# A flamingo layer stack on one core: the block-scale products of two roundings on GpSimd instead of VectorE

## The chip, the core and the metric

The kernel runs on one core of one Trainium2 chip. The metric is the device time of one execution in microseconds. The engines are named as the profile names them: PE is TensorE's matmul (PEld its weight load), DVE is VectorE, ACT is ScalarE, POOL is GpSimd, SP is SyncE, which here only issues DMAs.

## What is computed

Four layers in a row on 2048 tokens (4 x 512) of width 512, each with a residual and a tanh gain:

```python
x = x + tanh(g_xattn[0]) * L0_xattn(layernorm(x), token ids, ctx, ctx, ctx)   # 4 experts by token id
x = x + tanh(g_ffn[0])   * L0_ffn(layernorm(x), w_gate, w_up, w_down)          # block-float FFN
x = x + tanh(g_xattn[1]) * L1_xattn(layernorm(x), ctx, ctx, gamma)             # 8 heads of attention
x = x + tanh(g_ffn[1])   * L1_ffn(layernorm(x), ...)                           # 64-expert top-6 MoE
```

The change lies in the second layer. Its weights and its activations are rounded in blocks of 32 along the last axis:

```python
amax  = max(abs(block))                     # of 32 elements
scale = exp2(floor(log2(amax)) - 2)
q     = clip(round_to_tiny_float(block / scale), -max_norm, max_norm) * scale
...
gate, up = q_act(x) @ q_w(w_gate).T, q_act(x) @ q_w(w_up).T
out      = q_act(silu(gate) * up) @ q_w(w_down).T
```

The last step of either rounding, "times scale", is what is moved.

## The kernel before

The program has four stages that follow one another in time. In each of the first three, tiles are of 128 tokens and the order of the instructions on PE, ACT and DVE is the order in which the code emits them (a schedule written by hand); in the first two stages this holds for POOL's queue too[...].

**First layer and the rounding of weights (about 0 to 250 us).** Tokens are sorted by expert into 19 tiles. A loop over i (lines 531 to 558) transposes, multiplies with the context (`times_context`, L473), gates on DVE (`gated`, L485: one operand in SBUF, one in PSUM), scales on ACT (L489) and scatters the rows by an indirect DMA that POOL issues (`add_rows`, L490). For the first eight i, POOL also issues a gather (`take`, L441). Beside this, the generator `quantize` (from L240) rounds 24 blocks of weights of 128 x 1024, and each block is ten DVE instructions and a cast on ACT: a reduce to the block maxima (L247), two small integer operations on 128 x 32 (L249, L251), the division by the scale (L255), two operations for the exponent (L258, L260), two for rounding (L262, L265), the clamp (L268), and the product with `wide`, the scale spread over the block in bf16 by ACT at L253 (L270). The generator yields an assumed cost after every step, and `some_weights(us)` takes steps until that budget is used up: twice 3.6 us in each pass of the loop, some more ahead of it, and what is left after it. A block that is done goes into `rounded`, from which PE transposes it (L206 or L221) in a later `turn_weights`. So the yields decide where on DVE's queue a block's steps lie between the loop's L485.

**FFN in block float (about 250 to 515 us).** 16 tiles. For tile j, DVE does `times_up` (L655) for four quarters, and `block_scales` and `block_round` for three pieces: the two halves of the hidden row (128 x 1024, called a0 and a1 here) and the next tile's normalized row h (128 x 512). `block_scales` is a reduce (L586) and two small operations (L587, L589), with a cast on ACT (L591); `block_round` is a product with the inverse scale into fp8 (L602), the clamp (L608) and the product with the scale (L609). PE transposes each piece (`turned`, L621), ACT copies it out of PSUM (L622), and then PE multiplies: `gate_up` (L641), `down` (L661). After a1 of three of the tiles, DVE also does `factors_from` (L158 and a chain of small operations). POOL issues one DMA per tile (L667).

The order on DVE in a tile is: L655 x2, scales and rounding of a0, scales and rounding of the next h, L655 x2, scales and rounding of a1.

**Attention and routing (about 515 to 850 us), MoE (about 850 us to the end).** The change touches no instruction of these. The attention stage starts when the FFN's buffers are free, and the first loads of expert weights (L756 to L759) are issued inside it. In the attention stage POOL has some small arithmetic of its own: L905 to L908 on 128 x 1, L1028 and L1034 on 128 x 64.

Of the kernel before, what the change touches and what calls it, by code (L numbers as in the profile page):

```python
# [14 lines left out]
ALU = mybir.AluOpType  # L15
# [31 lines left out]
def flamingo_kernel(  # L47
# [21 lines left out]
    nc = tc.nc  # L69
# [115 lines left out]
    with (  # L185
# [43 lines left out]
        sources, rounded = deque(), deque()  # L229

        def fetch_weights(n):
            for _ in range(n):
                if left:
                    f, args = left.popleft()
                    sources.append(f(*args))

        def quantize():


            n = 2 * D  # L240
            nb = n // BLK
            magic = 1.5 * 2.0 ** (23 - 1)
            while sources:
                src, turn = sources.popleft()
                s3 = src.rearrange("p (k b) -> p k b", b=BLK)
                top = qp.tile([P, nb], F32, name="mx_top")
                nc.vector.tensor_reduce(top, s3, AX.X, ALU.max, apply_absolute_value=True)  # L247
                yield 1.21
                nc.vector.tensor_scalar(top.bitcast(I32), top.bitcast(I32), EXP_MASK, None, ALU.bitwise_and)  # L249
                inv = qp.tile([P, nb], F32, name="mx_inv")  # L250
                nc.vector.tensor_scalar(inv.bitcast(I32), top.bitcast(I32), -1.0, float(254 << 23), ALU.mult, ALU.add)  # L251
                wide = qp.tile([P, n], BF16, name="mx_wide")
                nc.scalar.copy(wide.rearrange("p (k b) -> p k b", b=BLK), top.unsqueeze(2).to_broadcast([P, nb, BLK]))  # L253
                yield 0.36
                nc.vector.tensor_tensor(s3, s3, inv.unsqueeze(2).to_broadcast([P, nb, BLK]), ALU.mult)  # L255
                yield 1.22
                e = qp.tile([P, n], F32, name="mx_e", bufs=1)
                nc.vector.tensor_scalar(e.bitcast(I32), src.bitcast(I32), EXP_MASK, None, ALU.bitwise_and)  # L258
                yield 0.69
                nc.vector.tensor_scalar(e, e, 0.25, None, ALU.max)  # L260
                yield 0.69
                nc.vector.scalar_tensor_tensor(src, e, magic, src, ALU.mult, ALU.add)  # L262
                yield 1.22
                q = qp.tile([P, n], BF16, name="w_q", bufs=3)
                nc.vector.scalar_tensor_tensor(q, e, -magic, src, ALU.mult, ALU.add)  # L265
                fetch_weights(1)
                yield 1.22
                nc.vector.tensor_scalar(q, q, 1.5, -1.5, ALU.min, ALU.max)  # L268
                yield 0.5
                nc.vector.tensor_mul(q, q, wide)  # L270
                rounded.append((turn, q))
                yield 0.69

        left = deque(blocks)
        weights = quantize()
# [24 lines left out]
        with tc.tile_pool(name="route0", bufs=1) as rp:  # L300
# [88 lines left out]
            wide = [P, NT, NS]  # L389
# [6 lines left out]
            for j in range(0, NT, 4):  # L396
                wide = [P, 4, P]
# [56 lines left out]
        def turned(i, what, name):  # L454
            a = stages[i].pop(what)
            ps = ps_t.tile([P, KC, P], F32, name="l0_ps", tag="t")
            for k in range(KC):
                nc.tensor.transpose(ps[:, k, :], a[:, bass.ts(k, P)], ident)
            aT = wp.tile([P, KC, P], F32, name=name)
            nc.scalar.copy(aT, ps)  # L460
            stages[i][name] = aT
# [102 lines left out]
    with (  # L564
# [10 lines left out]
        def load(j):  # L575
            xt = fp.tile([P, D], F32, name="xt", bufs=9)
            nc.sync.dma_start(xt, x_rows[bass.ts(j, P), :])
            stages[j]["x"] = xt

        def block_scales(j, what, n):  # L580

            nb = n // BLK
            src = stages[j][what]
            s3 = src.rearrange("p (k b) -> p k b", b=BLK)
            top = fp.tile([P, nb], F32, name="mx_top", tag=f"mx_top{nb}")
            nc.vector.tensor_reduce(top, s3, AX.X, ALU.max, apply_absolute_value=True)  # L586
            nc.vector.tensor_scalar(top.bitcast(I32), top.bitcast(I32), EXP_MASK, None, ALU.bitwise_and)  # L587
            inv = fp.tile([P, nb], F32, name="mx_inv", tag=f"mx_inv{nb}")
            nc.vector.tensor_scalar(inv.bitcast(I32), top.bitcast(I32), -1.0, float(250 << 23), ALU.mult, ALU.add)  # L589
            wide = fp.tile([P, n], BF16, name="mx_wide", tag=f"mx_wide{n}")  # L590
            nc.scalar.copy(wide.rearrange("p (k b) -> p k b", b=BLK), top.unsqueeze(2).to_broadcast([P, nb, BLK]))  # L591
            stages[j]["mx", what] = inv, wide

        def block_round(j, what, n):

            nb = n // BLK
            src = stages[j].pop(what)
            inv, wide = stages[j].pop(("mx", what))  # L600
            q = fp.tile([P, n], F8, name="mx_q", tag=f"mx_q{n}", bufs=1)
            nc.vector.tensor_tensor(  # L602
                q.rearrange("p (k b) -> p k b", b=BLK), src.rearrange("p (k b) -> p k b", b=BLK),
                inv.unsqueeze(2).to_broadcast([P, nb, BLK]), ALU.mult, saturate=False,
            )
            most = 7.5 / 64.0
            c = fp.tile([P, n], BF16, name="mx_c", tag=f"mx_c{n}")
            nc.vector.tensor_scalar(c, q, most, -most, ALU.min, ALU.max)  # L608
            nc.vector.tensor_tensor(c, c, wide, ALU.mult)  # L609
            stages[j]["q", what] = c  # L610

        def normal(j):
# [16 lines left out]
        def turned_hidden(j, half):  # L629
            if half == 0:  # L630
                stages[j]["iT"] = fp.tile([P, FI // P, P], BF16, name="iT")
            n = FI // 2
            turned(j, ("a", half), n, ps_a, stages[j]["iT"], half * (n // P))

        def gate_up(j, c):
            hT = stages[j]["hT"]
            got = []
            for wT in (wgT, wuT):
                ps = ps_g.tile([P, 512], F32, name="gu", tag="g")
                for k in range(KC):  # L640
                    nc.tensor.matmul(ps, hT[:, k, :], wT[:, k, bass.ts(c, 512)], start=k == 0, stop=k == KC - 1)  # L641
                got.append(ps)
            stages[j]["gu", c] = got

        def silu(j, c):

            half = c // 2
            if c % 2 == 0:
                stages[j]["a", half] = fp.tile([P, FI // 2], F32, name="inter")
            part = stages[j]["a", half][:, bass.ts(c % 2, 512)]  # L650
            nc.scalar.activation(part, stages[j]["gu", c][0], AF.Silu, scale=16.0)

        def times_up(j, c):
            part = stages[j]["a", c // 2][:, bass.ts(c % 2, 512)]
            nc.vector.tensor_mul(part, part, stages[j].pop(("gu", c))[1])  # L655

        def down(j):
            iT = stages[j].pop("iT")
            y = ps_y.tile([P, D], F32, name="y")
            for c in range(FI // P):  # L660
                nc.tensor.matmul(y, iT[:, c, :], wdT[:, c, :], start=c == 0, stop=c == FI // P - 1)  # L661
            stages[j]["y"] = y
# [42 lines left out]
        for j in range(NT):  # L705
            more = j + 1 < NT

            if j:
                turned_hidden(j - 1, 1)
            times_up(j, 0)  # L710
            times_up(j, 1)
            gate_up(j, 2)
            silu(j, 2)
            block_scales(j, ("a", 0), half_n)
            block_round(j, ("a", 0), half_n)
            gate_up(j, 3)
            silu(j, 3)
            if j:
                down(j - 1)
            if j + 8 < NT:  # L720
                load(j + 8)
            sums_of(j + 6)
            if j + 2 < NT:
                normal(j + 2)
            if more:
                block_scales(j + 1, "h", D)
                block_round(j + 1, "h", D)
            if j:
                add_rows(j - 1)
            if more:  # L730
                turned_rows(j + 1)
            turned_hidden(j, 0)
            if more:
                gate_up(j + 1, 0)
                silu(j + 1, 0)
            times_up(j, 2)
            times_up(j, 3)
            block_scales(j, ("a", 1), half_n)
            if more:
                gate_up(j + 1, 1)  # L740
                silu(j + 1, 1)
            block_round(j, ("a", 1), half_n)
            factors_from(j + 3)
# [28 lines left out]
    with (  # L772
# [304 lines left out]
        for n in range((NT + 5) * KC):  # L1077
            j, i = divmod(n, KC)
            turn = ((n - 1) // KC, (n - 1) % KC)
# [185 lines left out]
```

## Time and profile before

| | us |
|---|---|
| median of 3 runs | 1281.77 (1279.57 to 1284.02) |
| the profiled execution: its own time | 1287.6 |
| the profiled execution: span from first to last instruction | 1285.6 |
| busy in the span: PE / DVE / ACT / POOL | 1021.9 / 784.5 / 575.1 / 404.4 |
| mean granted TensorE clock | 0.922 |

Single instructions of the profile that the text refers to, in us: the product of a 128 x 1024 block on DVE 0.69 (L270 and L609), of a 128 x 512 row 0.42 (L609); a reduce of 128 x 1024 1.22; an indirect scatter's issue on POOL 2.1 in the mean (L490), a gather's 1.06 (L441).

How to read it: busy time is the time in which an engine had an instruction running. An average over the whole span says little here, since each stage has another limit; the tables by stage, the timeline of one tile and the waits say which engine is the last to be ready in a stage.

### The profile page before, as it was taken

What the parts mean: (1) busy time and instruction counts of PE and PEld (TensorE: products, weight loads), DVE (VectorE), ACT (ScalarE), POOL (GpSimd) and SP (SyncE); (2) the same over time, 40 slices, a digit from 0 to 9 for tenths busy, and PEclk for the clock granted to TensorE, in tenths of its full rate; (3) what the DMA queues carried; (4) which work ended last, traced back from release to release, by engine and by line L of the source; (5) the groups of instructions that cost most, each with busy time, mean ns of one, the idle gap of its engine ahead of it and who ended that gap; (6) DMA issues with size and microseconds to landing.
All of it is one profiled execution on the core that took longest, in us unless ns stands there. A gap on an engine that the chain in (4) does not pass through costs nothing. (4 is left out here: it accounts for less than half of the span.)

```text
span 1285.6 us, 14848 instructions
## 1 busy us (share of the span) xinstructions
PE 1021.9 (79%) x4603; PEld 524.6 (41%) x4603; DVE 784.5 (61%) x1965; ACT 575.1 (45%) x1144; POOL 404.4 (31%) x554
## 2 busy tenths in 40 slices
PE   4498889358878888588999999994499999999930
PEld 3244444123433333244455555452255555554410
DVE  7799999769999997547677776664122222222200
ACT  3766665366767564456565656551011111111100
POOL 3033312100000000013454535357244544444324
PEclk9799999769999998689999999997699999999975
DMA  9844444311111111972222222129699999999978
GB/s 329 296 102 112 93 96 82 85 31 33 33 17 18 19 23 17 267 209 59 64 64 68 52 60 43 44 38 243 165 286 276 278 276 270 272 265 274 275 199 137
DMA packets 78109, 178.94 MB, mean 139 GB/s; under 512 B 13280, under 2 KB 14320, under 8 KB 77968
## 3 DMA queue, kind: packets, MB, share of 16 engines
q1 hardware_dynamic: 51696, 128.04, 32.8%
q0 software_dynamic: 25504, 49.35, 21.3%
q8 instruction: 37, 0.61, 0.2%
q10 hardware_dynamic: 832, 0.62, 0.2%
q14 instruction: 40, 0.33, 0.1%
HBM read 133.76 MB, written 48.40 MB: 142 GB/s over the span
## 5 line engine op out<-in xcount | busy, mean ns | idle before, releaser
L1174 PE MATMUL gu_ps<-e_gu,gT 128*96 128x384 f32 x512 | 178.5, 492 | 3.5 <-DMA e_gu<-in_L_ffn_w_up_dram 2.2
L836 DVE TENSOR_REDUCE low<-at_s 128x2 f32<-128x1024 f32 x64 | 78.1, 1222 | 87.8 <-PE at_s L831 85.5
L845 ACT ACTIVATE p<-at_s,low 128x512 f32<-128x512 f32 x128 | 86.8, 684 | 87.6 <-DVE low L836 72.4
L1178 DVE SCALAR_TENSOR_TENSOR a<-s,xg,gu_ps 96x192 f32<-96x192 f32 x64 | 35.1, 548 | 147.0 <-ACT s L1176 144.7
L1197 PE MATMUL e_y<-e_dn,eaT 96*96 96x512 f32 x256 | 120.5, 592 | 0.5 <-ACT e_o L1199 0.5
L125 POOL DMA_INDIRECT taken<-token_no,to_i x96 | 97.2, 1013 | 46.8 <-issue 24.7
L1174 PEld LDWEIGHTS gu_ps<-e_gu,gT 128*96 128x96 f32 x512 | 79.2, 165 | 66.6 <-issue 63.7
L1176 ACT ACTIVATE s<-gu_ps 96x192 f32<-96x192 f32 x64 | 20.9, 326 | 178.0 <-PE gu_ps L1174 175.3
L1166 DVE COPY gT<-g_ps 128x384 f32<-128x384 f32 x64 | 35.6, 558 | 104.1 <-PE g_ps L1164 66.8
L667 POOL DMA_DIRECT2D x_rows<-y_sb x16 | 13.9, 868 | 260.6 <-ACT y_sb L666 260.6
L1151 POOL DMA_INDIRECT xg<-h_rows,idx x64 | 59.6, 931 | 93.9 <-DVE a L1178 62.0
L490 POOL DMA_INDIRECT x_rows<-y_sb,to_row x19 | 40.5, 2132 | 147.7 <-ACT y_sb L489 147.7
L831 PE MATMUL at_s<-c_tile,q 64*128 64x512 f32 x256 | 75.6, 670 | 13.7 <-DMA c_tile<-in_ctx_dram 13.7
L856 ACT COPY pT<-p_ps 128x512 f32<-128x512 f32 x128 | 70.1, 591 | 34.5 <-PE p_ps L855 34.2
L855 PE MATMUL p_ps<-ident,p 128*128 128x128 f32 x512 | 72.9, 281 | 14.1 <-ACT pT L856 12.1
L855 PEld LDWEIGHTS p_ps<-ident,p 128*128 128x128 f32 x512 | 57.7, 142 | 61.1 <-issue 26.4
L641 PEld LDWEIGHTS <-hT 128*128 128x128 bf16 x512 | 49.7, 101 | 69.6 <-issue 11.9
L1199 ACT COPY e_o<-e_y 96x512 f32<-96x512 f32 x64 | 37.2, 581 | 89.8 <-PE e_y L1197 84.2
L641 PE MATMUL gu<-wgT,hT 128*128 128x512 bf16 x256 | 70.1, 399 | 6.4 <-ACT hT L622 6.4
L473 PE MATMUL l_mm<-cT,hT 128*128 x152 | 70.9, 610 | 1.7 <-ACT hT L460 1.7
L473 PE MATMUL l_mm<-cT,sT 128*128 x152 | 72.1, 618 | 0.0
L641 PE MATMUL gu<-wuT,hT 128*128 128x512 bf16 x256 | 68.2, 390 | 1.9 <-DVE inter L655 1.9
(227 smaller groups left out, 2026.4 us busy)
## 6 DMA issues: line engine op xcount, KB each, us to landing
e_gu<-in_L_ffn_w_gate_dram SPq DMA_DIRECT2D x64, 384.0 KB
e_gu<-in_L_ffn_w_up_dram SPq DMA_DIRECT2D x64, 384.0 KB
e_dn<-in_L_ffn_w_down_dram SPq DMA_DIRECT2D x64, 384.0 KB
w_src<-in_L_ffn_w_gate_dram SPq DMA_DIRECT2D x8, 512.0 KB
c_sb<-in_ctx_dram SPq DMA_DIRECT2D x4, 1024.0 KB
w_src<-in_L_ffn_w_up_dram SPq DMA_DIRECT2D x8, 512.0 KB
more_rows<-zeros SPq DMA_DIRECT2D x16, 256.0 KB
w_src<-in_L_ffn_w_down_dram SPq DMA_DIRECT2D x8, 512.0 KB
```

What stands on the lines that cost most here:

```text
L125: ins = nc.gpsimd.indirect_dma_start(out=table[:, :], out_offset=bass.IndirectOffsetOnAxis(ap=to, axis=0), in_=what, in_offset=None)
L473: nc.tensor.matmul(ps.unsqueeze(1), aT[:, k, :], cT[:, bass.ds(at + k, 1), :], start=k == 0, stop=k == KC - 1)
L490: nc.gpsimd.indirect_dma_start(out=x_rows[:, :], out_offset=bass.IndirectOffsetOnAxis(ap=to_row[:, i : i + 1], axis=0), in_=y_sb[:, :], in ...
L641: nc.tensor.matmul(ps, hT[:, k, :], wT[:, k, bass.ts(c, 512)], start=k == 0, stop=k == KC - 1)
L831: nc.tensor.matmul(s[:, h, :], t["q"][rows, bass.ts(i, P)], t["c"][rows, :], start=True, stop=True)
L836: nc.vector.tensor_reduce(low, tiles[j]["s", i], AX.X, ALU.max, negate=True)
L845: nc.scalar.activation(p[:, h, :], s[:, h, :], AF.Exp, bias=low[:, h : h + 1], accum_out=t["sums"][:, i, h : h + 1])
L855: nc.tensor.transpose(ps[:, k, :], p[:, h, bass.ts(k, P)], ident)
L856: nc.scalar.copy(tiles[j]["pT"][h][:, :, bass.ts(i, P)], ps)
L1151: nc.gpsimd.indirect_dma_start(out=g[:, :], out_offset=None, in_=h_rows[:, :], in_offset=bass.IndirectOffsetOnAxis(ap=idx[:, e : e + 1], a ...
L1174: nc.tensor.matmul(ps, gT[:, k, :], gu[:, :, k, :], start=k == 0, stop=k == KC - 1)
L1197: nc.tensor.matmul(y, aT[:, c, :], dn[:, c, :], start=c == 0, stop=c == 1)
```

## The change

Both products with the block scale are issued by GpSimd (`nc.gpsimd`) instead of VectorE. In the weights' generator the product no longer has a yield of its own (the 0.69 goes), so a block counts 7.11 where it counted 7.80, and it is emitted together with the clamp. In the FFN loop the transposes of the second half of the tile before, `turned_hidden(j - 1, 1)`, are emitted on PE after `gate_up(j, 2)` instead of at the head of the tile.

```diff
                 nc.vector.tensor_scalar(q, q, 1.5, -1.5, ALU.min, ALU.max)
+
+                nc.gpsimd.tensor_mul(q, q, wide)
+                rounded.append((turn, q))
                 yield 0.5
-                nc.vector.tensor_mul(q, q, wide)
-                rounded.append((turn, q))
-                yield 0.69
...
             nc.vector.tensor_scalar(c, q, most, -most, ALU.min, ALU.max)
-            nc.vector.tensor_tensor(c, c, wide, ALU.mult)
+
+            nc.gpsimd.tensor_tensor(c, c, wide, ALU.mult)
             stages[j]["q", what] = c
...
-            if j:
-                turned_hidden(j - 1, 1)
             times_up(j, 0)
             times_up(j, 1)
             gate_up(j, 2)
             silu(j, 2)
+            if j:
+                turned_hidden(j - 1, 1)
             block_scales(j, ("a", 0), half_n)
             block_round(j, ("a", 0), half_n)
```

In the built program the order on the engines moves with it. POOL's queue in the first stage holds five products ahead of the first scatter, and then mostly one product per pass, between the scatters and gathers. On DVE the blocks of weights lie earlier against the loop: the last L485 comes after the last clamp L268, where before the change 2 blocks and more of rounding followed the last L485.

## What was predicted

> **What bounds the kernel now.** I read the table of busy times by stage first, then the groups of the first stage, then DVE's timeline in one FFN tile, then GpSimd's own arithmetic. The columns of the first table are stretch and length in us, then busy us of PE, PEld, DVE, ACT and POOL (each with a count), granted clock, DMA share, GB/s.
>
> ```profile
> 72.00:250.00 178.00, 150.16 (x574) 76.07 (x572) 167.90 (x267) 106.16 (x192) 49.46 (x27) 0.97 0.39 88
> 250.00:515.00 265.00, 202.55 (x1088) 94.72 (x1088) 226.18 (x438) 163.71 (x256) 13.63 (x16) 0.92 0.17 31
> 515.00:850.00 335.00, 292.17 (x1510) 158.20 (x1511) 222.70 (x782) 196.96 (x470) 126.59 (x279) 0.96 0.35 91
> 850.00:1285.60 435.60, 342.86 (x1274) 172.71 (x1272) 113.18 (x329) 70.63 (x157) 200.38 (x201) 0.90 0.94 239
> ```
>
> In the first stage DVE is busy 167.9 of 178 us (94%), PE 150; in the FFN, 226 of 265 with start and end included, and over 37 of every 40 us in the middle. The other two stages have other limits and follow the FFN's end, so what the first two lose or gain passes to the end one for one.
>
> ```profile
> L247 DVE TENSOR_REDUCE mx_top<-w_src 128x32 f32<-128x1024 f32 x19 | 23.0, 1213 | 0.0
> L255 DVE TENSOR_TENSOR w_src<-w_src,mx_inv 128x1024 f32<-128x1024 f32 x19 | 23.3, 1225 | 0.7
> L260 DVE TENSOR_SCALAR mx_e<-mx_e 128x1024 f32<-128x1024 f32 x20 | 13.9, 694 | 0.7
> L270 DVE TENSOR_TENSOR w_q<-w_q,mx_wide 128x1024 bf16<-128x1024 bf16 x20 | 13.9, 693 | 2.1
> ```
>
> The reader is to see 693 ns, what a block's product costs DVE, and that L260 takes about half of L255's time for as many f32 elements.
>
> ```profile
> 352.15 0.69 DVE L608 TENSOR_SCALAR mx_c<-mx_q 128x1024 bf16<-128x1024 fp8e4 x1
> 352.95 0.69 DVE L609 TENSOR_TENSOR mx_c<-mx_c,mx_wide 128x1024 bf16<-128x1024 bf16 x1
> 353.56 0.68 DVE L586 TENSOR_REDUCE mx_top<-h 128x16 f32<-128x512 f32 x1
> 354.27 0.17 DVE L587 TENSOR_SCALAR mx_top<-mx_top 128x16 int32<-128x16 int32 x1
> ...
> 355.42 0.43 DVE L608 TENSOR_SCALAR mx_c<-mx_q 128x512 bf16<-128x512 fp8e4 x1
> 355.95 0.42 DVE L609 TENSOR_TENSOR mx_c<-mx_c,mx_wide 128x512 bf16<-128x512 bf16 x1
> 356.29 1.28 DVE L655 TENSOR_TENSOR inter<-inter,gu 128x512 f32<-128x512 f32 x2
> ```
>
> DVE runs back to back: a tile takes 14.07 us (from L586 at 343.54 to L586 at 357.61), and 3.3 us more where the statistics chain L158 to L165 follows. With the gap ahead of it, a 1024-wide product occupies 0.80 of the tile, the 512-wide one 0.5.
>
> **What GpSimd takes, and what the two engines do to each other.**
>
> ```profile
> L905 POOL TENSOR_TENSOR r_t<-r_y x48: 192/193/194, 555.7 to 869.9; 128x1 f32<-128x1 f32 x48
> L1034 POOL TENSOR_TENSOR count<-count,chosen x14: 313/315/784, 611.4 to 879.9; 128x64 f32<-128x64 f32 x14
> ```
>
> ```profile
> 865.31 0.74 DVE L894 TENSOR_TENSOR x_tile<-x_tile,r 128x512 f32<-128x512 f32 x1
> 865.44 0.78 POOL L1034 TENSOR_TENSOR count<-count,chosen 128x64 f32<-128x64 f32 x1
> ```
>
> From 1 to 64 elements GpSimd's two-input operation grows by 122 ns, 1.94 ns an element, so 1024 elements are worked out at 193 + 1023 x 1.94 = 2.2 us and 512 at 1.2 us. The Trainium skill (GPSIMD Engine Reference, 3.1 Elementwise) states 4497 ns for 2048 f32, half of which is 2.25 us; the two agree. No bf16 product on POOL is in this trace. The last fence is the one meeting in it of a DVE operation with both inputs in SBUF and a GpSimd product: the latter, usually 0.31 us, took 0.78 and ended 0.17 after DVE's. The skill (SBUF — State Buffer, Who interferes with whom) says why: GpSimd's only port pair is DVE's second one, taken for a whole instruction, and whoever comes second waits, if DVE's is a two-port mode or has two SBUF inputs and GpSimd reads SBUF. A reduce and an operation with a PSUM input stay free. The reverse direction, DVE held by GpSimd, this trace doesn't show at any length. Which operations are in a two-port mode: VectorE: DVE Perf Modes, Mode 2×_2P, gives it to single-source SBUF operations; L260's 694 against L255's 1225 ns agrees. So of a weight block's remaining nine instructions only L247 is free of GpSimd, in the FFN only L586 and L655, and L485 in the first stage.
>
> **The change, part by part.**
>
> *First stage.* Removed from DVE: 24 x 0.73 us (0.693 and a gap) = 17.5. Added: 24 products on POOL, each from 0.15 (the handover of L1007 to L1034) to 2.35 us after the clamp's end. Behind the clamp DVE's queue has, by the built order: in 16 blocks L247 (1.25 us) and then a two-port operation, so DVE stands 1.1 us in each, 17.6; in 6 blocks also L485, cover 1.9, 0.45 each, 2.7; in one L158 at once, 2.3; in the last one nothing. Together 22.6. POOL's queue: where the clamp follows L485 closely, the product lies behind the scatter L490 (2.2 us, its row is ready with L485) and for early i the gather L441 (1.0), starts up to 2 us late and meets L249 to L258 rather than L247; I put some 4 us on this (0 to 10). Stalls 26.6. Cheaper yields also put the last L485 behind the last clamp; before, 20 us of rounding followed it and hid its path. Now that path is bare: L485's transposes 0.7, copy 0.6, weights' transposes 0.6, product with the context 2.6 to 3.5, L489 0.7, L490 2.2, handovers, landing (2, an estimate from the gap of 2.7 us between the loads' issue at 249.34 and ACT's start on their data at 252.03) make about 10.5, against 1.1 from the last product to 249.34 now: +9.4 (bounds 0 and 10). Sum: -17.5 + 26.6 + 9.4 = +18.5.
>
> *FFN.* Removed: 0.80 + 0.80 + 0.5 = 2.1 us of DVE per tile. Added stalls, from the end of a0's clamp as zero: the reduce of h ends at 0.7, L587 stands until 2.35, h's clamp ends at 4.0, its product runs from 4.2 to 5.4; L655 x2 and L586 cover that; a1's clamp ends at 8.9. PE gets h 1.35 us after its clamp instead of 0.5 (355.85 to 356.37): with 1.13 from product to first matmul (356.37 to 357.50) gate_up starts at 6.5 and its second pair ends 3.64 later, at 10.1, while DVE asks for it at 9.5: 0.65 more. L586 ends at 12.1, a1's product (to 11.3) is covered, and a0's clamp ends at 14.5: a tile of 14.47 for 14.07, +0.4. In the three tiles with statistics L158 stands until the product ends: +2.2. So 13 x 0.4 + 3 x 2.2 + the bare product at the first h (0.85) and the last a1 (1.55) = +14.2, less 0.8 in the last tile, which has no h after a0: +13.4. The moved `turned_hidden` costs nothing: it lets gate_up(j, 2) run while the product is under way; without it PE would stand another 1 to 2 us in front of it.
>
> *ACT, DMA.* The casts wait for a free `wide` until the product two back is read, far off. POOL's DMAs in the FFN (0.86 us each) have 13 us of idle time before them; a product ahead costs nothing.
>
> Sum +32 us: of the profiled execution's 1287.6 (span 1285.6, 2.0 around it) it makes 1319.5; the median of the runs lies 5.8 lower, so 1314.
>
> **Rivals.** *The pair isn't held against DVE (faster).* Then no stalls: first stage -17.5 + 9.4 = -8; in the FFN DVE asks for 12.0 a tile, and PE's own 12.4 (7.3 + 3.6 + 1.5) with the same loop through h gives about 12.85: 13 x -1.2, 3 x -2.1 and 2.4 at the ends, -19. Together -27: 1255. For it: no row shows DVE waiting for GpSimd. Against: L1034's 0.78. It decides from the first L249 behind a product.
>
> *Bf16 products are quicker than f32 ones.* With 1.3 us, L247 covers all but 0.2: first stage about -1, FFN about -12: 1269. Between -13 there and +32 at 2.2 us the line crosses nothing near 1.55 us. Against: in GpSimd's mask building a bf16 128x128 select took 328 ns and an f32 one 287, so width is no gain there.
>
> *The tail isn't bare or the queue does more:* 0 for 9.4 gives 1304, 10 for the 4 us of queueing 1320.
>
> **Chances.** Lock as worked out, whatever its tail: 0.62, slower, 1298 to 1330. No lock: 0.25, 1245 to 1272, faster. Shorter or partial holding, 1270 to 1298: 0.13, of which faster 0.05, same 0.05, slower 0.03. A measurement of this kernel tells about 0.3% (4 us) from nothing. Faster 0.30, same 0.05, slower 0.65. The range leaves out the lower part of the second case and ends at 1258 and 1330; the likeliest case's own range is 1298 to 1330.
>
> **What would show it.** POOL: 24 and 48 new products, about 2.2 us (1024) and 1.2 (512). DVE: an idle gap or a longer L249 and L587 of 1 to 1.6 us behind L247 and L586, L158 up to 2.3. A tile from 14.07 to about 14.5. The FFN's first load near 268 instead of 249. It would be wrong if L249 and L587 keep 0.18 us with no gap before them, or if products are well under 1.6 us.

## The result and the profile after

The changed kernel takes 1325.01 us (median of 4 runs, 1324.1 to 1335.13), the kernel before 1281.48 (median of 4, 1279.57 to 1284.02): a ratio of 1.0357, 95% interval 1.0323 to 1.0392 (the two medians alone give 1.034). It is slower; the forecast was 1314, with 1298 to 1330 for its likeliest case. The profiled execution took 1325.43, its span is 1323.3.

The same table by stage, with the stretches moved to where the stages now lie. (In all fences below, rows of the view that the reading doesn't need, mostly of other engines, are left out.)

```profile
72.00:250.00 178.00, 146.36 (x534) 74.41 (x533) 167.64 (x245) 100.14 (x182) 75.32 (x42) 0.94 0.37 83
250.00:275.00 25.00, 12.52 (x47) 5.59 (x46) 9.40 (x12) 6.69 (x11) 9.03 (x5) 0.88 0.30 51
275.00:540.00 265.00, 200.71 (x1036) 94.08 (x1037) 221.90 (x382) 156.53 (x249) 93.60 (x60) 0.88 0.15 29
```

VectorE is as busy as before, 167.6 of 178 us, but with 245 instructions where it had 267: part of the busy time is no work. The second line is a stretch of 25 us between the old end of the first stage and the new start of the FFN; VectorE is busy for 9.4 us of it. In the FFN the granted clock of PE is 0.88 where it was 0.92.

The groups of instructions show where VectorE's time went, and what the new products cost (from L609 on, lines of the changed kernel are one higher than before). The first fence is the kernel before, the second the changed one:

```profile
L249 DVE TENSOR_SCALAR mx_top<-mx_top 128x32 int32<-128x32 int32 x24 | 4.4, 183 | 0.8
...
L587 DVE TENSOR_SCALAR mx_top<-mx_top 128x16 int32<-128x16 int32 x16 | 2.8, 175 | 0.6
```

```profile
L587 DVE TENSOR_SCALAR mx_top<-mx_top 128x16 int32<-128x16 int32 x16 | 25.6, 1600 | 0.5
L249 DVE TENSOR_SCALAR mx_top<-mx_top 128x32 int32<-128x32 int32 x24 | 19.8, 823 | 0.7
...
L610 POOL TENSOR_TENSOR mx_c<-mx_c,mx_wide 128x1024 bf16<-128x1024 bf16 x32 | 67.8, 2120 | 138.5 <-ACT mx_wide L591 54.6 <-ACT inter L652 42.9 <-DVE mx_c L608 18.2
L270 POOL TENSOR_TENSOR w_q<-w_q,mx_wide 128x1024 bf16<-128x1024 bf16 x24 | 52.3, 2180 | 70.2 <-DVE w_q L268 61.5 <-ACT y_sb L489 7.6 <-DVE ln_mean L158 1.1
L610 POOL TENSOR_TENSOR mx_c<-mx_c,mx_wide 128x512 bf16<-128x512 bf16 x16 | 18.5, 1155 | 42.0 <-DVE mx_c L608 23.6 <-DVE ln_a L161 18.4
```

The two small operations took 175 ns (L587 on 128 x 16) and 183 ns (L249) and now take 1600 and 823 in the mean. Their work has not changed. No gap stands before them either (0.5 and 0.7 us in all): a VectorE instruction that can't proceed while GpSimd's product runs, called held here, appears as a long instruction and not as idle time, so a list of waits doesn't find it. The timeline of one tile shows it (VectorE and GpSimd alone):

```profile
381.13 0.69 DVE L608 TENSOR_SCALAR mx_c<-mx_q 128x1024 bf16<-128x1024 fp8e4 x1
381.74 0.68 DVE L586 TENSOR_REDUCE mx_top<-h 128x16 f32<-128x512 f32 x1
382.00 2.13 POOL L610 TENSOR_TENSOR mx_c<-mx_c,mx_wide 128x1024 bf16<-128x1024 bf16 x1 [3.53 <-ACT inter L652]
382.45 1.71 DVE L587 TENSOR_SCALAR mx_top<-mx_top 128x16 int32<-128x16 int32 x1
384.19 0.18 DVE L589 TENSOR_SCALAR mx_inv<-mx_top 128x16 int32<-128x16 int32 x1
384.40 0.69 DVE L602 TENSOR_TENSOR mx_q<-h,mx_inv 128x512 fp8e4<-128x512 f32 x1
385.13 0.43 DVE L608 TENSOR_SCALAR mx_c<-mx_q 128x512 bf16<-128x512 fp8e4 x1
385.48 1.28 DVE L656 TENSOR_TENSOR inter<-inter,gu 128x512 f32<-128x512 f32 x2
385.70 1.15 POOL L610 TENSOR_TENSOR mx_c<-mx_c,mx_wide 128x512 bf16<-128x512 bf16 x1 [1.57 <-DVE mx_c L608]
```

The product runs from 382.00 to 384.13. The reduce beside it keeps its 0.68 us; L587 ends at 384.16, at the moment the product does. The 512-wide product lies under L656, an operation with a PSUM input, which keeps its 1.28 us.

The end of the first stage:

```profile
259.03 0.68 DVE L485 TENSOR_TENSOR s<-s,l_mm 128x512 f32<-128x512 f32 x1
259.30 2.12 POOL L270 TENSOR_TENSOR w_q<-w_q,mx_wide 128x1024 bf16<-128x1024 bf16 x1 [3.15 <-DVE w_q L268]
...
261.93 3.65 PE L473 MATMUL l_mm<-cT,sT 128*128 x8
265.67 0.69 ACT L489 ACTIVATE y_sb<-l_mm,th 128x512 f32<-128x512 f32 x1 [2.69 <-issue]
266.80 1.57 POOL L490 DMA_INDIRECT x_rows<-y_sb,to_row  x1 [3.64 <-ACT y_sb L489]
272.41 1.75 SPq L577 DMA_DIRECT2D xt<-x_rows  x4
```

From the last L485's end (259.71) to the FFN's first load it is 12.7 us of one chain: it waits for the end of the last product (261.42), and then nothing of the rounding runs beside it. Such a chain is called bare here. Before, the first load came 1.1 us after the last product.

By stage, against the profile before (measured, forecast in brackets): the first FFN load 249.34 to 272.41, +23.1 (+18.5); from there to the attention stage's first load of rows 269.5 to 288.0, +18.5 (+13.4); from there to the end 766.8 to 762.9, -3.8 (0). Sum +37.8 (+32).

The profiles of the runs below show how far such a difference can be trusted. With the first stage as before, seven profiles have the first FFN load between 249.34 (this one, the earliest) and 251.62 us. With the FFN as before, four have it 266.0 to 270.1 us long. From the attention stage on, where no run changes anything, the fourteen profiles take 756.6 to 776.3 us; from the attention stage's first load to its last product it is 345.0 to 346.7, so most of the spread lies in the MoE. The two losses are clear of this, the -3.8 is not.

### The profile page after: what moved, and what is told of

Read it like the earlier page. It is cut to its first block, busy times and chain, and to the rows that moved or that the text cites. A ratio compares the mean times of both kernels' runs of the same rounds, so it can differ in the third digit from the quotient of the medians.

```text
span 1323.3 us, 14965 instructions
## 1 busy us (share of the span) xinstructions
PE 1035.9 (78%) x4603; PEld 532.0 (40%) x4603; DVE 797.2 (60%) x1893; ACT 573.8 (43%) x1144; POOL 535.0 (40%) x626
## 3 DMA queue, kind: packets, MB, share of 16 engines
q0 software_dynamic: 25504, 49.35, 20.4%
## 5 line engine op out<-in xcount | busy, mean ns | idle before, releaser
L610 POOL TENSOR_TENSOR mx_c<-mx_c,mx_wide 128x1024 bf16<-128x1024 bf16 (+1 forms) x48 | 86.3, 1798 | 180.4 <-ACT mx_wide L591 54.6
L1201 POOL DMA_INDIRECT out_dram<-e_o,idx x35 | 50.2, 1434 | 87.6 <-DMA out_dram<-e_o,idx 47.5
L622 PE MATMUL q_ps<-ident_bf,mx_c 128*128 128x128 bf16 x320 | 26.5, 236 | 72.8 <-POOL mx_c L610 72.8
L642 PEld LDWEIGHTS <-hT 128*128 128x128 bf16 x512 | 52.6, 107 | 74.9 <-issue 24.6
L642 PE MATMUL gu<-wgT,hT 128*128 128x512 bf16 x256 | 77.2, 430 | 5.3 <-ACT hT L623 5.3
L473 PE MATMUL l_mm<-cT,sT 128*128 x152 | 76.0, 646 | 6.1 <-ACT sT L460 6.0
L270 POOL TENSOR_TENSOR w_q<-w_q,mx_wide 128x1024 bf16<-128x1024 bf16 x24 | 52.3, 2180 | 70.2 <-DVE w_q L268 61.5
```

Of the source, the lines that this page charges most:

```text
L473: nc.tensor.matmul(ps.unsqueeze(1), aT[:, k, :], cT[:, bass.ds(at + k, 1), :], start=k == 0, stop=k == KC - 1)
L610: nc.gpsimd.tensor_tensor(c, c, wide, ALU.mult)
```

## Experiments

### Is it the hold? (twin)

The kernel before, in full, with a second product on GpSimd behind each of VectorE's, into a tile that nobody reads:

```diff
                 nc.vector.tensor_mul(q, q, wide)
+                twin = qp.tile([P, n], BF16, name="w_twin", bufs=1)
+                nc.gpsimd.tensor_mul(twin, q, wide)
...
             nc.vector.tensor_tensor(c, c, wide, ALU.mult)
+            twin = fp.tile([P, n], BF16, name="mx_twin", tag=f"mx_twin{n}", bufs=1)
+            nc.gpsimd.tensor_tensor(twin, c, wide, ALU.mult)
```

> The kernel before, with DVE's products left as they are, and behind each of them a GpSimd product of the same shape whose result nobody reads (extra work, 24 + 48 instructions). Theory (DVE is held while GpSimd's product runs): nothing is taken from DVE, so all stalls are added bare. First stage: in 17 blocks L247 covers 1.25 of 2.3 us, 1.1 each, in 6 a statistics chain follows at once, up to 2.3 each, so about +32; FFN: 15 x 1.5 behind a0 and 3 x 2.2 at the statistics, +29. About 1340 us, and DVE's small operations L249 and L587 show 1 to 1.7 us. Rival (it is the later hand-over of the product to PE that costs): nobody waits for the twin, so no change, 1282.

Measured: 1344.18 us (1341.08 to 1345.47) for 1284.78, ratio 1.0475 (1.044 to 1.0509); the first FFN load comes 32.8 us later and the FFN is 30.9 us longer. Nothing waits for the result of a twin. Against the profile before, VectorE's instructions in these two stages are 58.6 us longer in sum (29.9 and 28.7), while its open waits there stay near 31 us. So the hold accounts for the 59.4 us between the medians; the rival of this run (a late hand-over) and the prediction's rival without a hold fall. The groups of this kernel:

```profile
L249 DVE TENSOR_SCALAR mx_top<-mx_top 128x32 int32<-128x32 int32 x24 | 22.4, 935 | 0.8
L161 DVE SCALAR_TENSOR_TENSOR ln_a<-ln_a,ln_mean 128x4 f32<-128x4 f32 x7 | 12.0, 1719 | 0.2
```

L161 has 4 elements a row and took 162 ns before: how small an operation is doesn't save it from a hold.

### The two halves alone (weights_only, ffn_only)

weights_only is the change without the FFN's part:

```diff
-            nc.gpsimd.tensor_tensor(c, c, wide, ALU.mult)
+            nc.vector.tensor_tensor(c, c, wide, ALU.mult)
```

and with `turned_hidden` at the head of the tile as before. ffn_only is the change with the weights' generator as before.

> Only the weights' products go to GpSimd; the FFN is that of before. Theory: the first stage's end moves as in the changed kernel, +23, the rest not: 1304 us. Rival (the loss is in the FFN, where PE waits for its rows): 1281 to 1287.

> Only the activations' products go to GpSimd, with the moved transposes; the weights' rounding is that of before. Theory: FFN +18.5, of which stages behind it may give back up to 4: 1296 to 1300 us. If first stage and FFN act on one another (the clock, the loads), this and the run with only the weights' products won't add up to +43.

Measured: weights_only 1308.02 us, ratio 1.0193 (1.0159 to 1.0227), first FFN load at 271.64. ffn_only 1303.61, ratio 1.0142 (1.0101 to 1.0183), first load at 250.91, FFN 288.0 us long. Both are some 4 us above what was expected; the kernel before took 1284.78 beside them, 3.3 more than beside the change. Each half loses, and the excesses (1.9% and 1.4%) make nearly the whole 3.6%: the stages add up, as they follow one another.

### The first stage: order and product apart (weights_old_order, yield_only)

weights_old_order puts the yields back to what they were, with the weights' product on GpSimd and the FFN as before; yield_only does the opposite: every product on VectorE, only the yields as in the change.

```diff
weights_old_order, against the change:
                 nc.vector.tensor_scalar(q, q, 1.5, -1.5, ALU.min, ALU.max)
+                yield 0.5
                 nc.gpsimd.tensor_mul(q, q, wide)
                 rounded.append((turn, q))
-                yield 0.5
+                yield 0.69

yield_only, against the kernel before:
-                yield 0.5
                 nc.vector.tensor_mul(q, q, wide)
                 rounded.append((turn, q))
-                yield 0.69
+                yield 0.5
```

> Only the weights' products on GpSimd, as in the run with only the weights, but the generator yields 0.69 behind the product as before, so the last L485 again lies more than two blocks ahead of the last clamp. Theory (part of the first stage's loss is the path from the last L485 to the scatter, bare at the end): the scatter is hidden again, the first load of the FFN is issued some 2 to 4 us after the last product instead of 11 us, though more clamps have a statistics chain right behind them (5 for 3): 1299 to 1304 us, 4 to 9 below the run with the new order. Rival (only the stalls count): no better than that run, 1305 to 1312.

> The kernel before with all products on VectorE, where only the weights' generator is budgeted as in the change: product emitted with the clamp, its yield of 0.69 removed. It takes the order of the first stage apart from the engine of the product. Theory (the changed order leaves the last pass of the loop bare behind the last block): no stalls, DVE's work as before, but some 10 us of tail behind it, the FFN's first load near 259 to 262 and the time 1291 to 1296. Rival (the order is free, the 20 us are the product's alone): first load 250, 1280 to 1286.

yield_only: 1297.47 us (1285.09 to 1301.26), ratio 1.0102 (1.0026 to 1.0179), just above the 1291 to 1296 of the theory. Its profiled execution is its fastest (1285.09: in it the stages from attention on took 758.3 us, for 766.8 in the profile before). It has the first FFN load at 259.04, +9.7 us:

```profile
246.07 0.69 DVE L270 TENSOR_TENSOR w_q<-w_q,mx_wide 128x1024 bf16<-128x1024 bf16 x1
246.68 0.68 DVE L485 TENSOR_TENSOR s<-s,l_mm 128x512 f32<-128x512 f32 x1
...
253.58 1.55 POOL L490 DMA_INDIRECT x_rows<-y_sb,to_row  x1 [3.87 <-ACT y_sb L489]
259.04 1.28 SPq L577 DMA_DIRECT2D xt<-x_rows  x3
```

The reader is to see the same bare chain as in the changed kernel, 11.7 us from L485's end, without a single product on GpSimd. So the order that the smaller yield makes costs some 10 us by itself, read at the first load.

weights_old_order came out far from what was expected: 1333.57 us (1323.66 to 1335.13) where 1299 to 1304 stood, ratio 1.0359 (1.0294 to 1.0425), 25 us more than weights_only. The bare chain did go, as expected (last product starts at 288.77, first load at 292.05, 3.3 us); but everything ahead of it came later. One pass of its timeline (VectorE and GpSimd alone):

```profile
185.50 1.21 DVE L247 TENSOR_REDUCE mx_top<-w_src 128x32 f32<-128x1024 f32 x1
185.96 1.58 POOL L490 DMA_INDIRECT x_rows<-y_sb,to_row  x1 [6.87 <-ACT y_sb L489]
186.75 3.00 DVE L249 TENSOR_SCALAR mx_top<-mx_top 128x32 int32<-128x32 int32 x1
187.00 2.70 POOL L270 TENSOR_TENSOR w_q<-w_q,mx_wide 128x1024 bf16<-128x1024 bf16 x1
```

The clamp ended at 185.59 (L268, 185.16 and 0.43 long), but the product stands behind the scatter in GpSimd's queue. It starts 1.4 us later, 0.54 us before the scatter's own record ends, is recorded with 2.70 us instead of 2.12, and ends at 189.70 where 187.9 was possible. The reduce that should cover it is over, and L249 stands for 3.00 us. (L249 starts 0.25 us before the product's record and is held all the same; what holds it until then, the trace doesn't say.) Of the 24 products, 16 start directly behind a gather or a scatter, where in weights_only it is 6; ten are recorded with 2.46 to 2.73 us. PE waits 34.2 us for such products at L206 (14 waits, for 11.6 in 5), s then comes late to L485, and VectorE, which waits for no one in this stretch of weights_only, waits 11.9 us for ACT. VectorE's instructions are lengthened by 42.9 us in sum, for 28.7.

Read at the first load, the order of the change thus costs 9.7 us while the product is VectorE's, and saves 20.4 once it is GpSimd's (271.64 for 292.05; 25 us by the medians): the smaller yield moves most products out from behind the scatters.

### The FFN: is it the stalls, the path through h, or PE's clock? (ffn_swapped, ffn_warm, ffn_warm_twice)

In the change 16 tiles stall 1.5 us each in L587, some 23 us, while the ordinary tiles run in 14.32 to 16.01 where they took 14.06. Seven of eleven are longer than 14.32, by 1.1 to 1.7. In these seven, and in none of the four at 14.32, PE is slow after its wait for the product of h. That wait was 0.87 us before the change and is mostly 2.26 now; where the statistics precede it, it was 3.32 and is 4.88. PE before the change, then three times in the changed kernel, with two stretches of its table:

```profile
356.43 0.84 PE L621 MATMUL q_ps<-ident_bf,mx_c 128*128 128x128 bf16 x12 [0.87 <-DVE mx_c L609]
```

```profile
356.58 0.84 PE L622 MATMUL q_ps<-ident_bf,mx_c 128*128 128x128 bf16 x12 [2.27 <-POOL mx_c L610]
357.65 1.67 PE L642 MATMUL gu<-wgT,hT 128*128 128x512 bf16 x4 [0.23 <-ACT hT L623]
...
372.58 0.84 PE L622 MATMUL q_ps<-ident_bf,mx_c 128*128 128x128 bf16 x12 [2.26 <-POOL mx_c L610]
373.66 1.04 PE L642 MATMUL gu<-wgT,hT 128*128 128x512 bf16 x4 [0.23 <-ACT hT L623]
...
405.71 1.46 PE L622 MATMUL q_ps<-ident_bf,mx_c 128*128 128x128 bf16 x12 [4.88 <-POOL mx_c L610]
406.99 1.89 PE L642 MATMUL gu<-wgT,hT 128*128 128x512 bf16 x4
...
410.62 1.03 PE L642 MATMUL gu<-wuT,hT 128*128 128x512 bf16 x4
```

```profile
405.70:410.00 4.30, 4.29 (x22) 2.36 (x23) 3.38 (x5) 2.68 (x4) 0.76 (x1) 0.60 0.48 61
410.00:415.00 5.00, 5.00 (x31) 2.53 (x30) 3.44 (x6) 2.78 (x5) 2.11 (x1) 1.00 0.01 3
```

After 405.71 four matmuls take 1.89 us and later 1.03, at a granted clock of 0.60 and then 1.00. The Trainium skill (TensorE: Matmul & The Clock Gate, Part 1: The HAM clock gate) says that PE's clock is halved after an idle window of about 3.4 us and restored after a busy one, by windows that run freely. The length of the slow stretch fits: wherever it begins after a wait of 2.26 to 2.62 us, the first three groups of four matmuls take 4.85 or 4.86 us together instead of 3.10, and 1.75 us lost at half the clock is a stretch of about 3.5 us (an estimate from these durations). The length of the wait doesn't fit: ten waits of 2.26 or 2.27 us were followed by the full clock four times and by the low one six times, while of three waits of 3.32 us before the change one (at 373.79 there) left the clock full. That the outcome differs at one and the same wait would agree with windows that run freely; no run here varies their phase.

ffn_swapped puts two L656 behind a0's product, which takes most of the stall away, and leaves the path through h as it is. ffn_warm and ffn_warm_twice are ffn_only with transposes of the identity on PE, which nobody reads, in the wait for h, and then in the wait behind the statistics too:

```diff
ffn_swapped, against ffn_only:
             gate_up(j, 3)
             silu(j, 3)
+            times_up(j, 2)
+            times_up(j, 3)
             if j:
                 down(j - 1)
...
                 gate_up(j + 1, 0)
                 silu(j + 1, 0)
-            times_up(j, 2)
-            times_up(j, 3)
             block_scales(j, ("a", 1), half_n)

ffn_warm, in turned:
+            if what == "h":
+                for c in range(48):
+                    nc.tensor.transpose(ps[:, c % 4, :], ident_bf, ident_bf)

ffn_warm_twice, also ahead of gate_up(j, 2):
+            if j in (2, 6, 10):
+                ps = ps_a.tile([P, 8, P], BF16, name="q_ps", tag="q_ps1024")
+                for c in range(64):
+                    nc.tensor.transpose(ps[:, c % 8, :], ident_bf, ident_bf)
```

> The FFN's products on GpSimd, weights on VectorE in their old order, and in the FFN loop the second pair of L655 moved directly behind the rounding of a0, ahead of the next h. Theory (the path through h sets the tile, not the sum of stalls): the stall of L587 falls from 1.5 to about 0.35 us a tile, because two L655 cover a0's product, but gate_up gets h no earlier than before, so a tile stays at 14.3 to 15.5 and the time within 4 us of the 1303.6 of ffn_only: 1300 to 1308. Rival (only the stalls count): about 1.15 us a tile less, 1285 to 1290.

> The FFN part of the change alone, with 48 transposes of the identity on PE (extra work, their result is overwritten) ahead of the four of h, so that PE doesn't stand idle while it waits for h's product. Theory of the rest of the FFN's loss (in tiles of 15.4 to 16.0 us instead of 14.3 the clock granted to PE right after its wait is 0.6, and gate_up takes 1.9 us for four matmuls instead of 1.03): these tiles fall to about 14.4, some 10 us in the FFN: 1291 to 1297 us, and the clock stays at 1.0. Rival (those tiles are late for another reason, a buffer or ACT): 1301 to 1308, or more by the extra work.

> ffn_warm with 64 more unread transposes of the identity on TensorE ahead of the gate_up that waits behind each of the three statistics chains. Theory (what a tile costs above 14.5 us is TensorE at a low clock after its wait): the three tiles after the statistics fall from 16.6 to 16.9 us to about 14.6, and the whole by 6 to 7 us against ffn_warm's 1307.7: about 1300, no more than 1303. Rival (the low clock only moves to another tile, or the loss isn't the clock's): no change, 1305 to 1310.

ffn_swapped: 1302.26 us, ratio 1.0124 (1.0066 to 1.0183), against 1303.61 for ffn_only: the rival's 1285 to 1290 falls. Its L587:

```profile
L587 DVE TENSOR_SCALAR mx_top<-mx_top 128x16 int32<-128x16 int32 x16 | 7.8, 484 | 0.6
```

1.1 us of stall less in each of 16 tiles, 18 us together; yet its ordinary tiles take 14.32 to 16.5, and 14 tile periods in a row add up to 219.7 against 223.7, most of the 4 us in the three tiles with statistics (17.5 to 17.8 for 18.8 to 19.1). VectorE now waits openly for gate_up instead (L656, in these periods 29.9 us in 22 waits, for 16.0 in 18). A stall of VectorE is not time lost where PE waits for the same path.

ffn_warm: 1307.66 us, ratio 1.0177 (1.0121 to 1.0232); 1291 to 1297 was expected. The warmed tiles did come to 14.56 (those that had been at 16.0, and from below those at 14.31), but the three that come after the statistics rose from 15.4 to 15.6 to 16.6 to 16.9, and the 14 periods add up to 224.2. In those PE waits 3.6 us at another place, with nothing to keep it busy (lines of these two kernels are 3 higher in the FFN's helpers):

```profile
375.61 1.86 PE L645 MATMUL gu<-wuT,hT 128*128 128x512 bf16 x4 [3.61 <-DVE inter L659]
377.27 1.06 PE L625 MATMUL q_ps<-ident_bf,mx_c 128*128 128x128 bf16 x8
378.13 1.91 PE L645 MATMUL gu<-wgT,hT 128*128 128x512 bf16 x4
```

ffn_warm_twice: 1298.77 us (1296.05 to 1303.72), ratio 1.0108 (1.0046 to 1.0171), inside what was expected. The same place there:

```profile
371.26 1.03 PE L645 MATMUL gu<-wgT,hT 128*128 128x512 bf16 x4
...
372.32 1.02 PE L645 MATMUL gu<-wuT,hT 128*128 128x512 bf16 x4
373.18 0.61 PE L625 MATMUL q_ps<-ident_bf,mx_c 128*128 128x128 bf16 x8
373.63 1.03 PE L645 MATMUL gu<-wgT,hT 128*128 128x512 bf16 x4
```

Every ordinary tile but the first now takes 14.31 to 14.57, and the 14 periods add up to 216.9: 7 us less than ffn_only's 223.7 for PE work that computes nothing. That the long tiles are PE's clock is shown by the profiles, in which the FFN falls from 287.4 us in ffn_warm to 279.5; of the medians only this pair (8.9 us) stands clear of their spread.

### A version that is faster (ffn_h_first, order_only, paired, h_first_yield)

If VectorE has enough to do behind each clamp that GpSimd can't hold (the cover of the product), the product should be free. In the FFN there are two L655 and a reduce for each 1024-wide product. ffn_h_first has the weights as before and this order on VectorE in a tile (PE's in step with it):

```diff
ffn_only:    L655 x2, a0, h, L655 x2, a1 (then factors_from)
ffn_h_first: L655 x2, h, a0, L655 x2, a1's scales, (factors_from,) a1's rounding
```

order_only is the same order with all products on VectorE. paired adds to ffn_h_first every second weight product on GpSimd, with two L247 emitted behind it; h_first_yield is ffn_h_first with the yields of the change and the weights' products on VectorE.

> The FFN's products on GpSimd as in the run before, but DVE's order in a tile is rearranged so that each product has operations behind it that don't need the shared ports: L655 x2, the next h, a0, L655 x2, a1, with the statistics ahead of a1's rounding. Theory (what costs is only the cover that is missing): cover is 2.5 us behind a0, 2.1 behind a1, 1.2 behind h, so stalls fall from 1.5 + 0.4 to about 0.4 a tile, DVE asks for 12.4 us a tile and PE for about the same: 12.6 to 13.0 a tile for 14.07, and 2.1 less per statistics tile: 1260 to 1268 us. Rival (PE's clock or the path through h decides, not the stalls): 1282 to 1300.

> The rearranged order of the FFN, with all products on DVE as before. Theory (the gain of the rearranged run comes from taking 2.1 us a tile off DVE): DVE still asks for 14.07 us a tile, 1280 to 1287 us. Rival (the order itself gains, the place of the products doesn't matter): near the rearranged run's 1258.

> The rearranged FFN with its products on GpSimd, and in the weights' rounding every second block's product on GpSimd, behind its clamp the reduces of the next two blocks (cover 2.45 us); the other blocks' products stay on DVE. Theory: 11 x 0.73 us less on DVE in a stage that it bounds, less about 3 stalls of 2 us where a scatter is ahead of the product: 1252 to 1258 us for the rearranged run's 1258. Rival (the scatters in GpSimd's queue push most products out of their cover): 1260 to 1275.

> ffn_h_first with the weights' products on VectorE and the weights' generator budgeted as in the change (yield of 0.69 removed). Theory of the bare tail: 1267 to 1271, some 10 us more than ffn_h_first's 1258.4. Rival (the order is free): 1257 to 1261.

ffn_h_first: 1258.38 us (1256.23 to 1261.66), ratio 0.9802 (0.9764 to 0.984): 2% faster than the kernel before, a little below the expected 1260 to 1268. order_only: 1282.8, ratio 0.9987 (0.9965 to 1.0008): the order alone brings nothing, the gain is the products'. A tile of ffn_h_first, on VectorE and GpSimd:

```profile
380.93 0.69 DVE L608 TENSOR_SCALAR mx_c<-mx_q 128x1024 bf16<-128x1024 fp8e4 x1
...
381.54 1.44 DVE L656 TENSOR_TENSOR inter<-inter,gu 128x512 f32<-128x512 f32 x2
381.80 2.13 POOL L610 TENSOR_TENSOR mx_c<-mx_c,mx_wide 128x1024 bf16<-128x1024 bf16 x1 [1.27 <-ACT iT L623]
...
382.90 0.68 DVE L586 TENSOR_REDUCE mx_top<-h 128x16 f32<-128x512 f32 x1
383.61 0.34 DVE L587 TENSOR_SCALAR mx_top<-mx_top 128x16 int32<-128x16 int32 x1
```

Of the product's 2.13 us L587 sees 0.16; over the FFN L587 stands 3.3 us too long where it stood 23, and an ordinary tile takes 12.29 in the median (12.11 to 13.73) instead of 14.06: 1.8 of the 2.1 us that leave VectorE are kept. The FFN's length falls from 269.5 to 245.7.

paired: 1277.39 (1270.94 to 1291.11), ratio 0.9949 (0.9929 to 0.9968), outside both expectations and 19 us worse than ffn_h_first. Its trace is of the slowest of its 19 executions (1291.11), so only the order is read from it: the last L485 ends at 251.92, after the last product (249.13), where in ffn_h_first it ends at 229.03, 20 us before the last product. h_first_yield, which has the same fault of order and no weight product on GpSimd, takes 1273.28 (1267.29 to 1282.01), ratio 0.9914 (0.989 to 0.9938), with the first FFN load at 259.58 for 249.99. It is above its expectation of 1267 to 1271, but far from the rival's 1257 to 1261. So the bare chain can account for most of what paired lost; that it does was not isolated, and VectorE's instructions that are lengthened in paired's first stage (10.9 us in sum) are the other candidate.

## Why the prediction was right, by its steps

- *GpSimd's product at 2.2 and 1.2 us.* Right: 2.12 and 1.16. The figure of the Trainium skill (GPSIMD Engine Reference, 3.1 Elementwise), which is for f32, held for bf16 (half of its 4497 ns for 2048 elements, 2.25 us, taken as an estimate for 1024): the narrower type shows no gain, and the second rival falls with it.
- *The hold.* Right, in place and direction (SBUF — State Buffer, Who interferes with whom): L247, L586, L485 and L656 (L655 before) under a product keep their length, and whatever else starts under one is held to its end, single-source operations and also L161 and L262 with two SBUF inputs (up to 1.99 and 3.35 us). In the first stage the lengthened instructions sum to about 27 us, for 26.6.
- *The bare tail, +9.4.* Right: 9.7 in yield_only, though two differences cancel there: the chain is 11.7 us for 10.5, and it begins 0.9 us before the time at which the rounding ended before (247.36 for 248.21). The term that was too small is scatter to load: 5.5 us in yield_only and 5.6 in the changed kernel (266.80 to 272.41), where 4.2 stood (2.2 and 2). In the changed kernel the chain is 12.7.
- *The rest of the first stage.* -17.5 + 27 + 9.7 is 19.2 of the measured 23.1. The last product's own length is 0.8 of it (L485's end to L473 2.2 us, 1.4 in yield_only); the other 3 us were not located, and up to 2.3 of them can be the profile before, whose first stage is the shortest of seven.
- *The queue, 4 us of 0 to 10.* Not far off for the changed order, as far as the sum of the stalls shows. For the order before, weights_old_order shows that it would have been far more. The prediction had the new yield only as a cost (the tail); that it also spares most of the queueing, by which the change is some 20 us better than it would be, it didn't see.
- *An ordinary FFN tile, 14.47.* Near where PE's clock is full: 14.32, with the wait of VectorE for gate_up at 0.63 us, for 0.65. In seven of eleven it isn't full, which costs 10.0 us together. This is the step that failed: the working had gate_up at a constant 3.64 us for two pairs, and took for granted that PE's longer wait for h costs only its length. It also costs PE's clock, a term that was put at nothing.
- *The statistics tiles, +2.6 (0.4 and 2.2).* Too high: 17.36 to 18.78, +1.4. In these tiles L158 isn't held: the product waits for ACT's cast L591, starts 0.4 to 0.8 us after the clamp, and holds the fourth, fifth or sixth operation of the chain, by 1.85 to 1.89 us. And where it does, VectorE no longer waits 0.63 us for gate_up, so the two terms don't add up. 3 x 1.4 and the two terms of the ordinary tiles (10 x 0.26, 10.0, less 0.35 in the first) make the 16.5 us by which the 14 periods grew; the ends have the other 2.0, where 1.6 was forecast.
- *Nothing in the later stages.* They were 3.8 us shorter, which lies inside their spread from profile to profile (756.6 to 776.3 us). What makes that spread stays open.

Of the 11 us between 1314 and 1325.01, 5.8 are in the profile (+37.8 for +32): 4.6 in the first stage, 5.1 in the FFN (the clock's 10 less what was put too high) and -3.8 later. The other 5.4 come from the profile before: it was of an execution 5.8 above its median, the one after is of one 0.4 above. So the direction and the hold were forecast for the right reason; that the FFN's sum is off by 5 us and not by 10 is luck, since terms that were too high stood against one that was missing, and so are the -3.8.

## What to carry to other kernels

In this kernel a product moved from VectorE to GpSimd was free only as far as the instructions behind it on VectorE were reduces or had an input in PSUM: count their time against the product's (here 2.12 us for 128 x 1024), and reorder first; the FFN's products then gave 2% instead of taking 1.4%. Look for the hold in the lengths of small VectorE operations, not in the list of waits, and before a stall is counted as loss, ask whether another engine waits for the same thing, and whether that engine pays more than the wait, as PE did here with its clock. Where a product shares GpSimd's queue with scatters, or a budget decides the order, see where it comes to lie in the queue and what is last at the stage's end.

## What was not expected of the hardware

- A PE wait of 2.26 us can be followed by some microseconds at the low clock (the first four matmuls in up to 1.85 us for 1.04), and the tiles with such a stretch ran 1.1 to 1.7 us longer; unread transposes in the wait removed this, tile by tile.
- A GpSimd product directly behind a scatter is recorded with 2.70 to 2.73 us for 2.12 (nine times in weights_old_order). Its record starts 0.54 to 0.57 us before the scatter's ends, so it need not have run slower.
- A held VectorE instruction has the waiting inside its own recorded duration: 3.00 us for 128 x 32 integers, for 0.18.
